# Attention logits moved from TensorE head sums to VectorE on quarter-and-head partitions, with the residual placed in PSUM by ScalarE

## The chip, the cores and the metric

The kernel runs on one core of one Trainium2 chip. The metric is the device time of one execution in microseconds. All data are fp32. A single core runs here, so there is no second die to compare with; "state" says only whether a run was within 1.5% of the fastest of its kernel.

## The reference, cut to what matters

Two bottleneck blocks run one after the other over a batch of 16 images of 1024 channels and 32x32 pixels. The first contains local attention over 3x3 neighbours (8 channels per head, 32 heads), the second a 3x3 convolution.

```python
# block 1
h = relu(bn1(conv1x1(x, w_conv1)))               # 1024 -> 256
q = relu(bnq(conv1x1(h, wq))); k = relu(bnk(conv1x1(h, wk))); v = bnv(conv1x1(h, wv))
kp   = (unfold3x3(k) + pos_h + pos_w).reshape(b, HEADS, d, 9, h, w)
attn = softmax(einsum('bgdhw,bgdkhw->bgkhw', qh, kp), axis=taps)
out  = relu(bnatt(einsum('bgdkhw,bgkhw->bgdhw', unfold3x3(v), attn)))
x1   = relu(bn3(conv1x1(out, w_conv3)) + x)      # 256 -> 1024, residual
# block 2
t = relu(bn(conv1x1(x1, w1))); t = relu(bn(conv3x3(t, w2)))
y = relu(bn(conv1x1(t, w3)) + x1)                # 256 -> 1024, residual
```

## The kernel before

Per image TensorE (PE) goes through six stages: *last_conv* (256 to 1024, ends block 1), *reduce_one*, the first convolution of a later image, a *Winograd* 3x3 convolution, the q/k/v *projection* of the image two ahead, and *expand_last* (256 to 1024, ends block 2). Attention runs beside all this on VectorE (DVE) and ScalarE (ACT). The order of each engine's instructions is settled when the program is built: code yields in the source say how the two strands are traced, and the builder may reorder within the data dependencies.

The logits of a pair of taps: DVE multiplies on channel partitions, PE sums the 8 channels of a head, ACT moves the sums out of PSUM (an *eviction*).

```python
def sums(k0, nk, prods):
    pl = psl.tile([P, 2, JPIX], F32, tag="pl")
    for n in range(NW):
        for j in range(NJ):
            nc.tensor.matmul(pl[j*NH:(j+1)*NH, :nk, :], heads[:, n, :],
                             prods[n][:, :nk, j*JPIX:(j+1)*JPIX], start=(n == 0), stop=(n == NW-1))
    nc.scalar.activation(e[:, k0:k0+nk, :], pl[:, :nk, :], AF.Identity)
...
nc.vector.scalar_tensor_tensor(prod, kp_window, posf[:, n, k], q[:, n], ALU.add, ALU.mult)
...
tree(ALU.max, mx)                                   # over the 9 taps
nc.vector.tensor_tensor(e, e, mx.unsqueeze(1).to_broadcast(...), ALU.subtract)
nc.scalar.activation(e, e, AF.Exp)
```

Both expand stages add the residual on DVE after the matmuls:

```python
def expand_conv(b, wt, src, scale, shift):
    for o in range(NC):                              # 8 tiles of 128 output channels
        xt = xr[b, o]                                # the residual, loaded by DMA
        ps = psum.tile([P, HW], F32, tag="ps")
        ... 4 matmuls into ps, start=(n == 0) ...
        nc.vector.scalar_tensor_tensor(xt, ps, scale(o), xt, ALU.mult, ALU.add)
        nc.scalar.activation(xt, xt, RELU, bias=shift(o), scale=1.0)
        yield o
```

Values go from channel partitions to "quarter of the image, head" partitions by eight DMAs (`vc<-vh`) after the projection. In *expand_last* each tile's output store is followed by the load of a residual of the next image. All these DMAs are issued by one queue, SP's.

Of the kernel before, what the change touches and what calls it, by code (L numbers as in the profile page):

```python
# [12 lines left out]
P = 128  # L13
# [11 lines left out]
XSTREAM = 5  # L25
# [4 lines left out]
HALO = (JROWS + 2) * PW  # L30
G = P // HEAD_DIM
# [28 lines left out]
def sa_bottleneck_kernel(ctx: ExitStack, tc: tile.TileContext, x, w1t, wqkvt, w3t, u1t, u2t, u3t, params, out):  # L60
# [6 lines left out]
    hpool = ctx.enter_context(tc.tile_pool(name="hpool", bufs=4))  # L67
# [3 lines left out]
    psum = ctx.enter_context(tc.tile_pool(name="psum", bufs=3, space=bass.MemoryType.PSUM))  # L71
    psl = ctx.enter_context(tc.tile_pool(name="psl", bufs=2, space=bass.MemoryType.PSUM))
# [23 lines left out]
    uw = dram.tile([NU, P, NW, NU, WID], F32, tag="uw", name="uw")  # L96
    queue, ready = [], []

    def fetch(name, b):

        t = wpool.tile([P, 2048], F32, tag="w", name=f"{name}_{b}")
        if name[0] == "U":
            i = int(name[1])
            nc.sync.dma_start(t, uw[i].rearrange("p m j o -> p (m j o)"))
            ready.append((name, b, t.rearrange("p (m j o) -> p m j o", m=NW, j=NU)))
            return
        src, n = {
            "w1": (w1t, WID), "wqkv": (wqkvt, 3 * WID), "w3": (w3t, C), "u1": (u1t, WID), "u3": (u3t, C)
        }[name]
        chunks = src.shape[0] // P  # L110
        view = t[:, : chunks * n].rearrange("p (c n) -> p c n", n=n)
        nc.sync.dma_start(view, src.rearrange("(c p) n -> p c n", p=P))
        ready.append((name, b, view))
# [35 lines left out]
    pos = const.tile([P, NW, 3, 3], F32, tag="pos", name="pos")  # L149
    for n in range(NW):  # L150
        ph = col("L0_conv_pos_h", 3 * n, 3)
        pw = col("L0_conv_pos_w", 3 * n, 3)
        nc.vector.tensor_tensor(
            pos[:, n],
            ph.unsqueeze(2).to_broadcast([P, 3, 3]),
            pw.unsqueeze(1).to_broadcast([P, 3, 3]),
            ALU.add,
        )
    posf = pos.rearrange("p n i j -> p n (i j)")
# [3 lines left out]
    heads = const.tile([P, NW, NH], F32, tag="heads", name="heads")  # L163
    nc.gpsimd.memset(heads, 0.0)
    for n in range(NW):
        block = heads[:, n, n * G : (n + 1) * G]
        nc.gpsimd.memset(block, 1.0)
        for base, sign in ((0, 1), (HEAD_DIM - 1, -1)):
            nc.gpsimd.affine_select(
                out=block,  # L170
                in_=block,
                compare_op=ALU.is_ge,
                fill=0.0,
                base=base,
                pattern=[[-sign * HEAD_DIM, G]],
                channel_multiplier=sign,
            )

# [67 lines left out]
    def expand_conv(b, wt, src, scale, shift):  # L246

        for o in range(NC):
            xt = xr[b, o]
            ps = psum.tile([P, HW], F32, tag="ps", name="ps")  # L250
            for half in range(2):
                for n in range(NW):
                    nc.tensor.matmul(  # L253
                        ps[:, halves(half)],
                        wt[:, n, o * P : (o + 1) * P],
                        src[:, n, halves(half)],
                        start=(n == 0),
                        stop=(n == NW - 1),
                    )
            nc.vector.scalar_tensor_tensor(xt, ps, scale(o), xt, ALU.mult, ALU.add)  # L260
            nc.scalar.activation(xt, xt, RELU, bias=shift(o), scale=1.0)  # L261
            yield o
# [22 lines left out]
    hidden, queries, values, attended = {}, {}, {}, {}  # L285

    def project(b):

        wqkv = take("wqkv", b)
        h = hidden.pop(b)  # L290
        q = hpool.tile([P, NW, HW], F32, tag="h", name=f"q_{b}")
        for which, name, func in ((0, "bnq", RELU), (1, "bnk", RELU), (2, "bnv", AF.Identity)):
            for n in range(NW):
                ps = psum.tile([P, HW], F32, tag="ps", name="ps")
                at = which * WID + n * P
                for half in range(2):
                    for m in range(NW):
                        nc.tensor.matmul(  # L298
                            ps[:, halves(half)],
                            wqkv[:, m, at : at + P],  # L300
                            h[:, m, halves(half)],
                            start=(m == 0),
                            stop=(m == NW - 1),
                        )
                if which == 0:
                    dst, src = q[:, n, :], ps
                else:
                    dst, src = inside((kp, vh)[which - 1], n), rows(ps)
                nc.scalar.activation(  # L309
                    dst, src, func,  # L310
                    bias=col(f"L0_conv_{name}_b", n), scale=col(f"L0_conv_{name}_s", n),
                )
                yield
        more_weights()
        queries[b] = q

    def relay_values(b):


        vc = apool.tile([P, HEAD_DIM, HALO], F32, tag="vc", name=f"vc_{b}")  # L320
        for n in range(NW):
            flat = vh[:, n].rearrange("p r w -> p (r w)")
            for j in range(NJ):
                at = j * NH + n * G
                nc.sync.dma_start(
                    vc[at : at + G],
                    flat[:, j * JROWS * PW : j * JROWS * PW + HALO],
                )
        values[b] = vc

    def logits(b):

        q = queries.pop(b)
        e = apool.tile([P, KK, JPIX], F32, tag="e", name=f"e_{b}")

        def sums(k0, nk, prods):
            pl = psl.tile([P, 2, JPIX], F32, tag="pl", name="pl")
            for n in range(NW):
                for j in range(NJ):
                    nc.tensor.matmul(  # L340
                        pl[j * NH : (j + 1) * NH, :nk, :],
                        heads[:, n, :],
                        prods[n][:, :nk, j * JPIX : (j + 1) * JPIX],
                        start=(n == 0),
                        stop=(n == NW - 1),
                    )
            nc.scalar.activation(e[:, k0 : k0 + nk, :], pl[:, :nk, :], AF.Identity)

        before = None
        for k0 in range(0, KK, 2):  # L350
            nk = min(2, KK - k0)
            prods = []
            for n in range(NW):
                prod = ppool.tile([P, 2, HW], F32, tag="t", name="prod")
                for k in range(nk):
                    i, j = divmod(k0 + k, 3)
                    nc.vector.scalar_tensor_tensor(  # L357
                        rows(prod[:, k, :]),
                        kp[:, n, i : i + H, j : j + W],
                        posf[:, n, k0 + k : k0 + k + 1],  # L360
                        rows(q[:, n, :]),
                        ALU.add,
                        ALU.mult,
                    )
                prods.append(prod)
                yield 1.28 * nk
            sums(k0, nk, prods)
# [23 lines left out]
    def weighted(b):  # L391

        e, se = weights_of.pop(b)
        vc = values.pop(b).rearrange("p d (r w) -> p d r w", w=PW)
        acc = ppool.tile([P, HEAD_DIM, JPIX], F32, tag="t", name="acc")

        def by_row(t):
            return t.rearrange("p d (r w) -> p d r w", w=W)
# [19 lines left out]
        for n in range(NW):  # L418
            for j in range(NJ):
                at = j * NH + n * G  # L420
                nc.sync.dma_start(a[:, n, j * JPIX : (j + 1) * JPIX], acc[at : at + G])  # L421
# [5 lines left out]
        yield 2.3  # L427
# [5 lines left out]
    ATTEND = 2 * KK * 1.28 + 2.7 + 4.7 + 3.9 + 2.3 + (KK - 1) * 4.6 + 2.3  # L433

    def last_conv(b):
# [3 lines left out]
            lambda o: col("L0_conv_bn3_s", o), lambda o: col("L0_conv_bn3_b", o),  # L439
# [33 lines left out]
    def winograd_conv(b, forms, early):  # L473
# [7 lines left out]
        def products(u, v, js):  # L481
            ps = psum.tile([P, 2, NW * TILES], F32, tag="ps", name="ps")
            for at, j in enumerate(js):
                for n in range(NW):
                    for m in range(NW):
# [4 lines left out]
                            start=(m == 0),  # L490
                            stop=(m == NW - 1),
                        )
            return ps

        def by_row(ap):
# [3 lines left out]
        for i in range(NU):  # L499
# [14 lines left out]
            z = (even, odd)[i] if i < 2 else zpool.tile([P, NW * NT, W], F32, tag="z", name="z")  # L514
            for parity, op in enumerate((ALU.add, ALU.subtract)):
                nc.vector.tensor_tensor(
                    z[:, :, parity::2], by_row(both[parity]), by_row(outer[:, parity]), op
# [15 lines left out]
    def expand_last(b):  # L533

        behind = 2
        for o in expand_conv(
            b, take("u3", b), hidden_one.pop(b),
            lambda o: bn_inv[:, 2 * NW + o : 2 * NW + o + 1],
# [41 lines left out]
    def cycle(b):  # L580
        along(last_conv(b), 2.1)
# [11 lines left out]
        if b + 2 < B:  # L593
            along(project(b + 2), 3.0)
        side.finish()
        if b + 2 < B:
            relay_values(b + 2)
            side.start(attend(b + 2))
        along(expand_last(b), 2.1)
# [20 lines left out]
    relay_values(0)  # L620
    for _ in winograd_weights():
        pass
    for c in range(NC):
# [3 lines left out]
    along(first_conv(2), 3.4)  # L627
    along(project(1), 3.4)
    side.finish()
    relay_values(1)  # L630
# [43 lines left out]
```

## Time and profile before

| | before |
|---|---|
| median of the first comparison | 2785.47 us (2782.49 to 2790.90, 4 runs) |
| profiled span, granted PE clock | 2782.0 us, 0.991 |
| PE busy / idle | 2704.2 / 77.8 us |
| a steady batch | 169.58 us |
| first last_conv starts at | 161.74 us |
| idle PE inside steady batches | 13 starts of the Winograd stage, 1.8 us each |

The prediction below shows the lines. In a line of a timeline the columns are start, time to the end of the last of the group, engine, source line, operation, output and inputs, shape, count, and in brackets the idle time before the group and what ended it. PE is the bound: what does not shorten PE's list or close one of its gaps does nothing.

### The profile page before, as it was taken

How to read it: one execution, taken by the hardware profiler on the slowest of the kernel's cores; microseconds unless marked ns; L12 is line 12 of the kernel's file. 1: busy time of each engine (PE TensorE's matmuls, PEld its weight loads, DVE VectorE, ACT ScalarE, POOL GpSimd, SP SyncE). 2: the span in 40 equal slices, each digit the busy share in tenths (PEclk: the TensorE clock that was granted, in tenths of full speed). 3: DMA queues.
4: the chain of work that ended last, by engine and by line, in shares of the span. 5: the costliest groups of instructions: out<-in, count | busy, mean ns of one | idle time of the engine just before them, and what ended most of it. 6: DMA issues, size and time to landing. Idle time of an engine off the chain costs nothing.

```text
span 2782.0 us, 20993 instructions
## 1 busy us (share of the span) xinstructions
PE 2704.2 (97%) x8192; PEld 1347.8 (48%) x8192; DVE 1944.0 (70%) x1683; ACT 672.0 (24%) x659; POOL 5.0 (0%) x13
## 2 busy tenths in 40 slices
PE   7989999999999999999999999999999999999898
PEld 3435345454544646445464454645546454454545
DVE  3769885867759587595866858677685775958725
ACT  2122312223122221313223122231322313122222
POOL 0000000000000000000000000000000000000000
PEclk9999999999999999999999999999999999999998
DMA  8632645346462554625356353464524546144342
GB/s 313 180 66 72 186 133 157 105 135 184 132 181 82 142 161 147 186 78 151 136 163 171 111 154 115 147 173 135 169 97 139 172 133 196 58 121 152 116 141 91
DMA packets 149970, 395.18 MB, mean 142 GB/s; under 512 B 12912, under 2 KB 78448, under 8 KB 141680
## 3 DMA queue, kind: packets, MB, share of 16 engines
q1 hardware_dynamic: 147712, 387.24, 46.3%
q10 hardware_dynamic: 2160, 6.60, 0.6%
q8 instruction: 65, 1.06, 0.2%
q14 instruction: 33, 0.27, 0.0%
HBM read 283.43 MB, written 71.30 MB: 128 GB/s over the span
## 4 chain that ended last, share of the span: by engine, by line
PE 78%; DVE 13%; DMA 3%; SPq 3%; ACT 2%; issue 1%; ACTq 0%; DVEq 0%
PE ps L253 32%; PE ps L234 16%; PE ps L486 14%; PE ps L298 11%; PE pl L340 5%; DVE term L402 3%; DVE acc L414 3%; SPq L421 3%; DVE v L465 3%; DMA a<-acc 2%; DVE tv L460 1%; DVE acc L416 1%; ACT a L422 1%; DMA g<-in_u2t_dram 1%; ACT vh L447 1%
## 5 line engine op out<-in xcount | busy, mean ns | idle before, releaser
L486 PE MATMUL ps<-v,U 128*128 128x256 f32 x2048 | 454.0, 383 | 36.3 <-ACT h L270 23.8
L357 DVE SCALAR_TENSOR_TENSOR prod<-kp,pos,q 128x1024 f32<-128x1024 f32 x288 | 351.5, 1279 | 167.0 <-ACT kp L309 156.1
L253 PE MATMUL ps<-h,u 128*128 128x512 f32 x1024 | 455.1, 601 | 11.2 <-ACT h L525 11.2
L234 PE MATMUL ps<-x,w 128*128 128x512 f32 x1024 | 445.5, 595 | 11.1 <-DMA w<-in_w1t_dram 11.1
L253 PE MATMUL ps<-a,w 128*128 128x512 f32 x1024 | 453.1, 598 | 2.3 <-DVE r L260 2.3
L234 PE MATMUL ps<-r,u 128*128 128x512 f32 x1024 | 442.4, 592 | 0.0
L486 PEld LDWEIGHTS ps<-v,U 128*128 128x128 f32 x2048 | 391.7, 192 | 103.2 <-ACT h L270 29.0
L298 PE MATMUL ps<-h,wqkv 128*128 128x512 f32 x768 | 337.0, 599 | 10.6 <-ACT kp L309 7.2
L253 PEld LDWEIGHTS ps<-h,u 128*128 128x128 f32 x1024 | 193.8, 192 | 269.6 <-issue 234.4
L234 PEld LDWEIGHTS ps<-x,w 128*128 128x128 f32 x1024 | 195.2, 191 | 257.8 <-issue 256.8
L253 PEld LDWEIGHTS ps<-a,w 128*128 128x128 f32 x1024 | 191.6, 190 | 258.0 <-issue 238.3
L234 PEld LDWEIGHTS ps<-r,u 128*128 128x128 f32 x1024 | 194.4, 190 | 245.2 <-issue 240.8
L260 DVE SCALAR_TENSOR_TENSOR r<-ps,bn_inv,r 128x1024 f32<-128x1024 f32 x128 | 164.2, 1283 | 194.0 <-PE ps L253 194.0
L414 DVE TENSOR_TENSOR acc<-acc,term 128x2048 f32<-128x2048 f32 x128 | 292.4, 2284 | 0.5
L402 DVE TENSOR_TENSOR term<-e,vc 128x2048 f32<-128x2048 f32 x128 | 289.9, 2283 | 0.0
L298 PEld LDWEIGHTS ps<-h,wqkv 128*128 128x128 f32 x768 | 147.5, 192 | 191.7 <-issue 178.7
L261 ACT ACTIVATE r<-r,bn_sh 128x1024 f32<-128x1024 f32 x128 | 146.7, 1148 | 346.8 <-DVE r L260 346.7
L465 DVE TENSOR_TENSOR v<-tv 128x512 f32<-128x512 f32 x256 | 160.4, 686 | 76.1 <-DMA a<-acc 74.8
L260 DVE SCALAR_TENSOR_TENSOR r<-ps,par,r 128x1024 f32<-128x1024 f32 x128 | 161.3, 1269 | 49.5 <-PE ps L253 25.2
L261 ACT ACTIVATE r<-r,par 128x1024 f32<-128x1024 f32 x128 | 145.3, 1144 | 182.2 <-DVE r L260 182.1
L340 PE MATMUL pl<-prod,heads 128*32 128x512 f32 (+1 forms) x1280 | 139.8, 555 | 0.0
L507 DVE TENSOR_TENSOR m<-m,ps 128x512 f32<-128x512 f32 x128 | 82.2, 683 | 81.6 <-ACT m L503 81.6
(61 smaller groups left out, 926.9 us busy)
## 6 DMA issues: line engine op xcount, KB each, us to landing
x<-in_x_dram SPq DMA_DIRECT2D x128, 512.0 KB, 3.3
r<-in_x_dram SPq DMA_DIRECT2D x128, 512.0 KB, 5.4
U<-uw SPq DMA_DIRECT2D x64, 1024.0 KB, 5.1
out_dram<-r SPq DMA_DIRECT2D x128, 512.0 KB, 5.9
vc<-vh SPq DMA_DIRECT2D x128, 170.0 KB, 10.7
w<-in_w1t_dram SPq DMA_DIRECT2D x16, 1024.0 KB, 7.8
w<-in_w3t_dram SPq DMA_DIRECT2D x16, 1024.0 KB, 4.9
u<-in_u1t_dram SPq DMA_DIRECT2D x16, 1024.0 KB, 7.5
```

The costliest lines, as they stand in the source:

```text
L234: nc.tensor.matmul(ps[n][:, halves(half)], wt[:, c, n * P : (n + 1) * P], src[:, halves(half)], start=(c == 0), stop=(c == NC - 1),)
L253: nc.tensor.matmul(ps[:, halves(half)], wt[:, n, o * P : (o + 1) * P], src[:, n, halves(half)], start=(n == 0), stop=(n == NW - 1),)
L260: nc.vector.scalar_tensor_tensor(xt, ps, scale(o), xt, ALU.mult, ALU.add)
L261: nc.scalar.activation(xt, xt, RELU, bias=shift(o), scale=1.0)
L298: nc.tensor.matmul(ps[:, halves(half)], wqkv[:, m, at : at + P], h[:, m, halves(half)], start=(m == 0), stop=(m == NW - 1),)
L340: nc.tensor.matmul(pl[j * NH : (j + 1) * NH, :nk, :], heads[:, n, :], prods[n][:, :nk, j * JPIX : (j + 1) * JPIX], start=(n == 0), stop=(n ...
L357: nc.vector.scalar_tensor_tensor(rows(prod[:, k, :]), kp[:, n, i : i + H, j : j + W], posf[:, n, k0 + k : k0 + k + 1], rows(q[:, n, :]), A ...
L402: nc.vector.tensor_tensor(by_row(dst), rows(e[:, k, :]).unsqueeze(1).to_broadcast([P, HEAD_DIM, JROWS, W]), vc[:, :, i : i + JROWS, j : j ...
L414: nc.vector.tensor_add(acc, acc, t)
L421: nc.sync.dma_start(a[:, n, j * JPIX : (j + 1) * JPIX], acc[at : at + G])
L465: nc.vector.tensor_tensor(v[:, j].rearrange("p n (r w) -> p n r w", w=NT), t[:, :, :, j0 : j0 + 2 * NT - 1 : 2], t[:, :, :, j1 : j1 + 2 * ...
L486: nc.tensor.matmul(ps[:, at, n * TILES : (n + 1) * TILES], u[:, m, j, n * P : (n + 1) * P], v[:, j, m, :], start=(m == 0), stop=(m == NW - 1),
```

## The change

The intent: take the head sums off PE. Query and key are moved to quarter-and-head partitions as the values were, so that a head's 8 channels lie along the free axis and DVE can multiply and add them itself. The position term becomes four differences per head (two rows and two columns relative to the last), computed by four matmuls on PE per image and added on DVE. The residual is put in PSUM by ScalarE ahead of the matmuls (a *seed*), and the scales are multiplied into the weights once, at the start. PSUM goes from 3+2 to 4 buffers. Smaller changes come along: 4 instead of 5 buffers for the input, 3 instead of 4 for `h`, and the attention of one image is finished before the projection of a later one begins. The core of the diff, cut:

```diff
-    psum = ... bufs=3 ...; psl = ... bufs=2 ...
+    psum = ... bufs=4 ...
-    def expand_conv(b, wt, src, scale, shift):
+    def expand_conv(b, wt, src, shift):
+        ahead = []
+        def seed(o):
+            if o < NC:
+                ps = psum.tile([P, HW], F32, tag="ps", name="ps")
+                nc.scalar.activation(ps, xr[b, o], AF.Identity)
+                ahead.append(ps)
+        seed(0)
+        seed(1)
         for o in range(NC):
-            ps = psum.tile(...)
+            ps = ahead.pop(0)
             ... matmuls ...
-                        start=(n == 0),
+                        start=False, skip_group_check=True,
-            nc.vector.scalar_tensor_tensor(xt, ps, scale(o), xt, ALU.mult, ALU.add)
-            nc.scalar.activation(xt, xt, RELU, bias=shift(o), scale=1.0)
+            nc.scalar.activation(xr[b, o], ps, RELU, bias=shift(o), scale=1.0)
+            seed(o + 2)
...
     def project(b):
+        # q, k and v to quarter-and-head partitions, each as soon as it is evicted: 8 DMAs each
+                for j in range(NJ):
+                    nc.sync.dma_start(by_head(halo, n, j), flat[:, ...])
+        # 4 position matmuls (64 columns each), evicted by ScalarE and moved by 4 DMAs
...
     def logits(b):
-        ... products on channel partitions, head sums on PE, eviction on ScalarE ...
+        for k in range(KK):
+            nc.vector.tensor_tensor(by_row(t), by_row(qc), kc[:, :, i:i+JROWS, j:j+W], ALU.mult)
+            nc.vector.tensor_add(t[:, 0:4], t[:, 0:4], t[:, 4:8])
+            nc.vector.tensor_add(t[:, 0:2], t[:, 0:2], t[:, 2:4])
+            nc.vector.tensor_add(e[:, k, :], t[:, 0], t[:, 1])
+            yield 4.6
+        ... two adds of the position terms, broadcast over rows and columns of taps ...
```

## The prediction

> **What bounds the kernel now.** I read the page first, then the timeline of one batch on each engine, then busy time by stage, then the waits.
>
> ```profile
> span 2782.0 us, 20993 instructions
> PE 2704.2 (97%) x8192; PEld 1347.8 (48%) x8192; DVE 1944.0 (70%) x1683; ACT 672.0 (24%) x659; POOL 5.0 (0%) x13
> ...
> PE 78%; DVE 13%; DMA 3%; SPq 3%; ACT 2%; issue 1%; ACTq 0%; DVEq 0%
> ...
> L486 PE MATMUL ps<-v,U 128*128 128x256 f32 x2048 | 454.0, 383 | 36.3 <-ACT h L270 23.8
> L357 DVE SCALAR_TENSOR_TENSOR prod<-kp,pos,q 128x1024 f32<-128x1024 f32 x288 | 351.5, 1279 | 167.0 <-ACT kp L309 156.1
> ...
> L340 PE MATMUL pl<-prod,heads 128*32 128x512 f32 (+1 forms) x1280 | 139.8, 555 | 0.0
> ```
>
> PE's busy time is 97% of the span: its idle time is at most 78 us, 60 by my count of gaps. So a saving is either PE work or one of those gaps; DVE (70%) and ACT (24%) matter only where PE waits for them. The granted clock is 0.991.
>
> A steady batch takes 169.58 us (projection starts at 1112.88 and 1282.46), and thirteen of the sixteen batches are such. PE's timeline of one:
>
> ```profile
> 1112.88 20.76 PE L298 MATMUL ps<-h,wqkv 128*128 128x512 f32 x48
> 1133.48 10.46 PE L253 MATMUL ps<-h,u 128*128 128x512 f32 x24
> 1143.87 1.92 PE L340 MATMUL pl<-prod,heads 128*32 128x512 f32 x16
> 1145.73 7.13 PE L253 MATMUL ps<-h,u 128*128 128x512 f32 x16
> ...
> 1258.18 24.44 PE L486 MATMUL ps<-v,U 128*128 128x256 f32 x112 [1.82 <-ACT h L270]
> ```
>
> Starts differ by 20.60 us for 48 projection matmuls: 429 ns each is the true pitch (the "mean 600 ns" overlaps). The head sums stand in PE's stream; 16 take 1.86 us. The one idle gap is 1.82 us at the start of the Winograd stage. On ACT, 25.40 us of waiting for the a<-acc transfers and then two a-activations (1252.09 to 1257) stand ahead of the evictions of h that PE wants.
>
> The queue and DMA decide one step below:
>
> ```profile
> 1134.09 5.15 SPq L325 DMA_DIRECT2D vc<-vh  x7
> 1141.25 5.55 SPq L541 DMA_DIRECT2D out_dram<-r  x3
> 1153.89 0.34 SPq L88 DMA_DIRECT2D r<-in_x_dram  x1
> ...
> 1133.48:1163.40 29.92, 29.92 (x94) 12.14 (x93) 20.21 (x17) 9.33 (x10) 0.00 (x0) 1.00 0.94 229
> ```
>
> The first residual of the next batch is issued 12.6 us after the first output store, because the store must land first; in that stage the DMA share is 0.94.
>
> [...] 16 instructions in 1.86 us, 116 ns each, against 429. [...] At N = 2048 [...] the trace has 2284. [...] the rows with pointers have 1148 (from SBUF) and 1195 to 1209 (from PSUM), so I take 1.15 us. [...]
>
> **The change part by part.**
>
> *Head sums leave PE.* 80 instructions per batch, 8.77 us of PE by stage sums, 16 batches: -140 us.
>
> *Position products join it.* Per batch 4 fp32 matmuls, each two instructions as everywhere in this trace: 8 x 429 ns / 2 side by side = 1.7 us, plus about 0.3 for switching: 2.0 x 16 = +32 us. The weight scaling at the start adds 32 instructions of 128 columns, a quarter of 429 each: +4.
>
> *DVE's work is exchanged, not cut.* Out: 351.5 us of prod and 164.2 + 161.3 = 325.5 us of the residual adds, together 677, or 42.3 per batch. In, per tap: 2.28 (2048 wide) + 1.22 + 0.69 + 0.42 = 4.6 us, nine times 41.4, plus two position adds of 1.76: 44.9. DVE goes from 120.35 to about 123 us per batch. But attention can no longer begin at 11.5 us into the projection: it must wait for q and k to be moved to the new partitions. The k transfers are like the vc ones (170 KB, 10.7 us to landing), the last issued about 18 us in: start at about 27. DVE then has some 135 us for 123: it fits, with attention ending near the end of the next first conv, as now (a<-acc issued at 1245.20, first conv ends at 1252.75).
>
> *ACT.* Seeds 16 x 1.15 = 18.4, less head-sum evictions (43.5/16 = 2.7), plus 1.2 for positions: 41.4 becomes 59 us per batch. In an expand stage it is relu 1.2 + seed 1.15 = 2.35 us per 3.43 us tile. It fits. Every tile is seeded two ahead with four PSUM buffers, so I expect no wait inside a stage.
>
> *Waits removed.* The a-activations are placed 15 us later and there is a fourth PSUM buffer: the 1.8 us gap goes, 13 x 1.8 = 24 us. The 7.24 us wait of the second projection for kp goes too. -31 us.
>
> *Waits gained, start.* Attention of batch 0 begins 74 us in rather than 59.6 and takes 41.4 + 3.5 + 2.9 + 2.5 + 3.5 (exp, table) + 4.5 + 37.7 + 2.2, about 98 us: 172. The transfers and activations of a add 11: the first last_conv starts at 183 instead of 161.7. +22 us.
>
> *Waits gained, each batch.* DMA work in and after the projection rises: 1024 packets of 1 KB for q (6.7 us of all 16 engines, as a<-acc takes), 1024 of 1360 bytes for k (11.5, as vc), 512 for positions (3.3). It begins at 5 us, where DMA is idle now (share 0.19 in the projection), but with vc and a weight load the backlog lasts to about 46 us instead of 38. So the first store lands at about 49 us instead of 41 and residual 0 at about 53. Now the residual is wanted after a tile's matmuls, afterwards before them: seed 0 of the next last_conv is wanted at 50 and done at 54. I choose 4 us for 13 batches: +52.
>
> *Sum.* 2782 - 140 + 36 - 31 + 22 + 52 - 1 (the last tile loses its DVE step) = 2720; the unprofiled median is 2.8 us above the profiled span: **2723 us**, 2.2% less.
>
> **The rivals.**
> (a) *No wait on seeds*: the transfers fit in the idle DMA of the projection. For it: the share of 0.19 there. Against: 0.94 right after. Without the 52 us: about 2670.
> (b) *Seeds and relus collide on ACT*: if the seeds of a stage queue behind the last eviction of the stage before, PE waits 1.2 + 1.15 + about 0.2 us at each of 32 stage starts, +83 us; about 2805 with (c)'s wait, 2755 in its place. Against: ACT is mostly idle, and instruction order here already differs from the source (a first term stands inside the tree of sums), so seeds can be placed early.
> (c) *ACT blocks on exp*: ACT is in order; if exp was placed for an earlier DVE than the real one (k lands late), relus and seeds of last_conv stand behind it. Now exp waits only 2.1 us for DVE. 3 us a batch would be +40 us: 2763.
> (d) *DVE becomes the bound*: 123 of 165 us, idle only while k is moved. If k lands 10 us later than I think, Winograd forms come late and PE waits up to that long: near 2800.
>
> **Range and chances.** With all head-sum savings kept and no new wait in the batches it is 2670; a little less if the start costs less: low 2655. With one more wait of 5 to 6 us a batch it is about 2795. The 2% border, 2729, lies next to my figure; (a) pulls down, (b) to (d) up, and the change looks tuned as a whole (yields, buffers), which favours (a). Faster 0.52, within 2% 0.43, slower 0.05.
>
> **What would show it.** PE busy about 2600 us and no head sums; projection plus positions about 22.5 us; DVE about 123 us a batch with an idle stretch of about 25 us from the Winograd end until k lands; last_conv of a steady batch starting with a wait of about 4 us on a seed that waited for r<-in_x_dram; the first last_conv at about 183 us; no wait on h at the Winograd start; a batch of about 164.5 us instead of 169.6. It is wrong if a batch takes 161 (no seed wait) or above 168 (stage-start or exp waits on ACT), or if the position products run one after another (3.4 us a batch, +24 us).

## The result, and the profile after

The changed kernel took 3200.30 us (3196.59 to 3202.18, 4 runs), against 2785.47 for the kernel before in the same rounds: ratio 1.1485, 95% interval 1.1464 to 1.1506. Ratios in this document are the mean time of one kernel's fast runs over the mean of the other's of the same rounds, so not quite the ratio of the medians quoted. The time is far outside the predicted range.

From the page of the changed kernel (in a group's line: busy time, mean ns of one, then the engine's idle time just before the group and what ended most of it):

```profile
span 3198.2 us, 19613 instructions
...
PE 2632.5 (82%) x7072; PEld 1347.0 (42%) x7072; DVE 1959.8 (61%) x1771; ACT 893.6 (28%) x851; POOL 5.0 (0%) x11
...
L289 PE MATMUL ps<-a,w 128*128 128x512 f32 x1024 | 476.3, 628 | 442.5 <-ACT ps L280 442.5
L407 DVE TENSOR_TENSOR prod<-qc,bnk 128x2048 f32<-128x2048 f32 x144 | 323.9, 2287 | 423.4 <-DMA bnk<-kp 252.7
...
L435 ACT ACTIVATE e<-e 128x2304 f32<-128x2304 f32 x16 | 34.0, 2122 | 432.8 <-DVE e L434 432.8
```

PE's busy time fell by 71.7 us, and still the span rose by 416.2, so PE's idle time rose by 487.9. Of that, 442.5 us stand in one row: *last_conv*'s matmuls waiting for ScalarE's seeds. And ScalarE waited almost the same total, 432.8 us, for DVE ahead of exp. The timeline of one batch shows how the two belong together. First PE:

```profile
1326.62 1.94 PE L379 MATMUL ps<-q,pos 128*64 128x512 f32 x8
...
1335.46 27.63 PE L289 MATMUL ps<-h,u 128*128 128x512 f32 x64
1394.04 29.13 PE L289 MATMUL ps<-a,w 128*128 128x512 f32 x64 [30.95 <-ACT ps L280]
```

*expand_last* ends at 1363.1, and *last_conv* begins 30.95 us later. ScalarE in that stretch:

```profile
1363.18 1.11 ACT L297 ACTIVATE r<-ps,bn_sh 128x1024 f32<-128x1024 f32 x1 [2.38 <-PE ps L289]
1390.95 2.12 ACT L435 ACTIVATE e<-e 128x2304 f32<-128x2304 f32 x1 [26.65 <-DVE e L434]
1392.98 2.90 ACT L280 ACTIVATE ps<-r 128x1024 f32<-128x1024 f32 x3
```

After the last ReLU of *expand_last* ScalarE's next instruction is exp; it stands there for 26.65 us until DVE has finished the logits, and only then do three seeds run, at once. DVE, meanwhile, started its logits late and then never paused:

```profile
1343.77 4.50 DVE L407 TENSOR_TENSOR prod<-qc,bnk 128x2048 f32<-128x2048 f32 x2 [28.23 <-DMA bnk<-kp]
...
1388.36 2.56 DVE L434 TENSOR_TENSOR e<-e,mx 128x2304 f32<-128x2304 f32 x1
```

It waited 28.23 us for the keys, and the subtraction that exp needs ended at 1390.9. The residuals were not the cause: in SP's list the first of them is issued at 1363.44, behind the eight values and three output stores,

```profile
1338.87 8.84 SPq L369 DMA_DIRECT2D bnv<-vh  x8
...
1350.29 3.42 SPq L595 DMA_DIRECT2D out_dram<-r  x3
1363.44 0.34 SPq L88 DMA_DIRECT2D r<-in_x_dram  x1
```

and the trace has it landed at 1367.74, some 25 us before the first seed ran.

The built order of ScalarE's instructions agrees (not a profile; a piece of the list of ACT instructions in the program built from the changed kernel):

```
L297 Activation r_6_2396<-ps,bn_sh 128x1024
L297 Activation r_7_2398<-ps,bn_sh 128x1024
L435 Activation e_2862<-e_2862 128x2304
L280 Activation ps<-r_0_2889 128x1024
L280 Activation ps<-r_1_2904 128x1024
```

Exp is ahead of every seed of the next *last_conv*, and ScalarE keeps to its list: in those 26.65 us it ran none of the seeds, although the residual of the first was there from 1367.74.

**The bill.** PE idle: +442.5 at *last_conv* (one wait of 39.1, thirteen of 30.6 to 32.0), +71.5 in the start (88.8 us of waits against 17.3), -23.7 for the thirteen Winograd waits, which are gone. (The first wait for weights, 11 to 12 us in both, is left out of the start.) Together +490, against +487.9 measured from busy times. PE busy: -71.7. A steady batch takes 194.0 us.

There is a smaller cost inside PE's busy time. Here are the wait, the *last_conv* after it and the next stage (columns: stretch, its length, busy PE, PEld, DVE, ACT and POOL, each with its count, then the granted clock, the DMA share and GB/s):

```profile
1362.00:1394.00 32.00, 1.08 (x3) 0.19 (x1) 29.71 (x28) 4.17 (x4) 0.00 (x0) 0.57 0.75 288
1394.00:1423.00 29.00, 28.96 (x64) 12.84 (x65) 29.00 (x17) 14.41 (x14) 0.00 (x0) 0.95 0.00 1
1423.00:1450.50 27.50, 27.50 (x66) 12.18 (x65) 2.92 (x2) 2.32 (x2) 0.00 (x0) 1.00 0.11 38
```

64 matmuls of one shape take 29.0 us after the wait and 27.5 one stage on, and the clock is 0.95 against 1.00. The trace's clock record stands at half from 1366.17, 3.1 us after the last matmul, to 1396.89, 2.9 us after the first one. In that slow beginning matmuls start 854 ns apart, afterwards 429. The ends of matmuls are modelled, so this is a reading of starts.

### The profile page after: what moved, and what is told of

The parts are those of the page before. It is cut to its first block, busy times and chain, and to the rows that moved or that the text cites. A ratio compares the mean times of both kernels' runs of the same rounds, so it can differ in the third digit from the quotient of the medians.

```text
span 3198.2 us, 19613 instructions
## 1 busy us (share of the span) xinstructions
PE 2632.5 (82%) x7072; PEld 1347.0 (42%) x7072; DVE 1959.8 (61%) x1771; ACT 893.6 (28%) x851; POOL 5.0 (0%) x11
## 5 line engine op out<-in xcount | busy, mean ns | idle before, releaser
L289 PE MATMUL ps<-a,w 128*128 128x512 f32 x1024 | 476.3, 628 | 442.5 <-ACT ps L280 442.5
L407 DVE TENSOR_TENSOR prod<-qc,bnk 128x2048 f32<-128x2048 f32 x144 | 323.9, 2287 | 423.4 <-DMA bnk<-kp 252.7
L289 PEld LDWEIGHTS ps<-a,w 128*128 128x128 f32 x1024 | 206.0, 203 | 712.6 <-ACT ps L280 454.7
L260 PE MATMUL ps<-x,w 128*128 128x512 f32 x1024 | 448.7, 598 | 38.2 <-DMA x<-in_x_dram 26.7
L510 DVE TENSOR_TENSOR tv<-vh 128x1088 f32<-128x1088 f32 x64 | 82.4, 1287 | 460.1 <-ACT vh L497 459.5
L453 DVE TENSOR_TENSOR term<-e,bnv 128x2048 f32<-128x2048 f32 x128 | 289.9, 2284 | 0.0
L280 ACT ACTIVATE ps<-r 128x1024 f32<-128x1024 f32 x256 | 257.5, 1021 | 13.8 <-DVE m L558 3.8
L297 ACT ACTIVATE r<-ps,par 128x1024 f32<-128x1024 f32 x128 | 142.6, 1114 | 244.9 <-PE ps L289 184.8
L297 ACT ACTIVATE r<-ps,bn_sh 128x1024 f32<-128x1024 f32 x128 | 142.5, 1113 | 203.4 <-PE ps L289 203.4
L410 DVE TENSOR_TENSOR prod<-prod 128x1024 f32<-128x1024 f32 x144 | 170.3, 1220 | 0.0
L435 ACT ACTIVATE e<-e 128x2304 f32<-128x2304 f32 x16 | 34.0, 2122 | 432.8 <-DVE e L434 432.8
```

The lines of the kernel that those rows point to most:

```text
L260: nc.tensor.matmul(ps[n][:, halves(half)], wt[:, c, n * P : (n + 1) * P], src[:, halves(half)], start=(c == 0), stop=(c == NC - 1),)
L280: nc.scalar.activation(ps, xr[b, o], AF.Identity)
L289: nc.tensor.matmul(ps[:, halves(half)], wt[:, n, o * P : (o + 1) * P], src[:, n, halves(half)], start=False, stop=(n == NW - 1), skip_grou ...
L297: nc.scalar.activation(xr[b, o], ps, RELU, bias=shift(o), scale=1.0)
L407: nc.vector.tensor_tensor(by_row(t), by_row(qc), kc[:, :, i : i + JROWS, j : j + W], ALU.mult)
L410: nc.vector.tensor_add(t[:, 0:4], t[:, 0:4], t[:, 4:8])
```

## The experiments

All give correct results but for one that is meant not to (said there). Each was run beside the kernel before on the same chip.

### 1. Exp queued behind the seeds

Theory A: exp's place in ScalarE's list makes the wait. Rival B: the seeds wait for something of their own (residuals, PSUM buffers), and exp only hides it. Edit: exp is made to stand behind the newest seed that has been traced.

```diff
+                newest[0] = nc.scalar.activation(ps, xr[b, o], AF.Identity)   # in seed()
...
-        nc.scalar.activation(e, e, AF.Exp)
+            with tc.issue_after(newest[0].ins):
+                nc.scalar.activation(e, e, AF.Exp)
```

> Edit: exp is queued on ACT behind the newest seed that was traced before it; nothing else. Theory (order): the 31 us wait of each last_conv is ACT standing at exp, in front of the seeds, until DVE has finished the logits. Then the wait falls to what the residual transfers leave, about 5 to 7 us (residual 0 lands 55 us after the projection's start, the stage could start at 50, plus a seed of 1.0); a batch takes 166 to 169 us instead of 194 and the kernel about 3200 - 14 x 26 = 2835 us (2800 to 2870). Rival (transfers): the seeds themselves come late because of the added relays; then the wait stays over 20 us and the kernel over 3080. Rival (late attention): the wait moves to the next point that needs attention; a batch stays over 185.

Measured: 2848.02 us, ratio 1.0238 (1.0213 to 1.0264): 352 us of the 415 between the medians came back with this one edit, as the theory expected. The waits at *last_conv* fell from 442.5 to 95.8 us in all. ScalarE at such a start:

```profile
1400.74 1.11 ACT L299 ACTIVATE r<-ps,bn_sh 128x1024 f32<-128x1024 f32 x1 [2.38 <-PE ps L291]
1405.74 1.03 ACT L282 ACTIVATE ps<-r 128x1024 f32<-128x1024 f32 x1 [3.88 <-DMA r<-in_x_dram]
...
1428.36 2.12 ACT L441 ACTIVATE e<-e 128x2304 f32<-128x2304 f32 x1 [3.54 <-DVE e L436]
```

Exp still comes when DVE is ready, but nothing that PE wants is behind it. What remains, 5.7 to 7.4 us a batch, is B: the seed waits 3.88 us for its residual. That is the wait that I had predicted, and it was hidden below the greater one.

### 2. No seeds at all

The residual is added by DVE in both stages, as before the change, but the rest of the change stays. If seeds are the fault, this should give the gain without the wait.

```diff
-        seed(0); seed(1)
-            ps = ahead.pop(0)            ... start=False
-            nc.scalar.activation(xr[b, o], ps, RELU, ...); seed(o + 2)
+            ps = psum.tile(...)          ... start=(n == 0)
+            nc.vector.tensor_tensor(xt, ps, xt, ALU.add)
+            nc.scalar.activation(xt, xt, RELU, bias=shift(o), scale=1.0)
```

> Edit: residual added by VectorE after the matmuls in both expand stages, as before the change (scales stay folded into the weights, all else of the change stays). ACT still has exp ahead of the relus of last_conv. Theory (order): PE no longer waits for ACT at last_conv, so that wait goes to 0; the relus stand behind exp, so a wait comes at reduce_one, which reads them: exp is ready about 78 + 10 us (eight adds ahead of it on DVE) after the projection's start and reduce_one could start at 77.5, so 10 to 16 us. A batch 171 to 179, kernel 2890 to 3000. Rival (relays and late attention are the cost, seeds are innocent): a batch stays at 185 to 194, kernel over 3080.

Measured: 3316.07 us, ratio 1.1912 (1.1894 to 1.1930), slower than the change itself: a clear miss. A batch takes 201.3 us. By its number the rival's forecast (over 3080 us) came true; the lines show what the wait is. PE in one batch:

```profile
1608.32 13.90 PE L280 MATMUL ps<-a,w 128*128 128x512 f32 x32
1661.40 15.78 PE L280 MATMUL ps<-a,w 128*128 128x512 f32 x32 [39.19 <-DVE r L287]
```

DVE's timeline there:

```profile
1654.24 2.56 DVE L424 TENSOR_TENSOR e<-e,mx 128x2304 f32<-128x2304 f32 x1
1658.99 1.23 DVE L416 TENSOR_TENSOR tree<-e 128x1024 f32<-128x1024 f32 x1 [2.19 <-ACT e L425]
1660.13 1.22 DVE L287 TENSOR_TENSOR r<-ps,r 128x1024 f32<-128x1024 f32 x1
```

PE fills the four PSUM buffers (32 of its 64 matmuls) and stops for 39.19 us, because the residual adds now stand in DVE's list behind the whole logits. It is the same fault on another engine: a short instruction that PE wants, behind a long chain that began late. Taking the seeds away does not take away the late start of the logits.

### 3. Seeds in expand_last only

*last_conv* adds on DVE, *expand_last* keeps its seeds, and exp is tied behind the newest ReLU. Edit: `seeded` is passed to the two stages as False and True, with the add of experiment 2 where it is False.

> Edit: seeds stay in the last expand stage; last_conv adds its residual on VectorE; exp is queued behind the newest relu traced before it. Theory (order plus late residuals): both parts of the wait go, the exp in front of the seeds and the residual that is wanted a tile earlier; a batch takes 161 to 164 us, kernel 2745 to 2800, level with the kernel before, because the start still loses about 75 us more than before. Rival (DVE becomes the bound with 133 us a batch and a late start): batch over 168 with waits at the Winograd stage for forms, kernel over 2840.

Measured: 2993.59 us, ratio 1.0753 (1.0737 to 1.0769). A miss again, with half the wait. PE's timeline in one batch:

```profile
1325.11 15.48 PE L292 MATMUL ps<-a,w 128*128 128x512 f32 x32 [16.09 <-DVE r L301]
```

DVE's timeline there:

```profile
1321.36 2.56 DVE L440 TENSOR_TENSOR e<-e,mx 128x2304 f32<-128x2304 f32 x1
1323.84 4.61 DVE L301 TENSOR_TENSOR r<-ps,r 128x1024 f32<-128x1024 f32 x4
```

Four adds stand behind the subtraction, which ends the logits. I had not asked, before either run, where the adds would stand in DVE's list; the bracket answers it. With seeds, only exp has to be moved out of the way; with adds, the logits themselves.

### 4. The start reworked

On top of experiment 3: the weight scaling takes residual buffers instead of those of the products, the first projection is traced after the preparation of the Winograd weights, and the residuals of batch 0 are loaded after the second image's first convolution.

```diff
+        diag = rpool.tile([P, NC, P], F32, tag="r", name="diag")      # one buffer for all 8 diagonals
...
-    along(project(0), 0.0)          # ahead of the Winograd weights
+    along(project(0), 0.0)          # behind them
-    for c in range(NC): load_residual(0, c)
     side.start(attend(0)); along(first_conv(1), 3.4)
+    for c in range(NC): load_residual(0, c)
```

> Edit: e3, and at the start the Winograd weights are traced before the first projection, the scaled weights use the residual buffers instead of the product buffers, and the first residuals are loaded after the second first_conv. Theory: the start loses 15 us to scaled weights that wait for a buffer, 27 us to input loads behind residual loads in the queue, and attention 0 starts 22 us late; the first last_conv begins near 185 us instead of 216, and the kernel is 25 to 45 us faster than e3: 2700 to 2770. Rival (the start is bound by attention 0 alone): under 10 us gained.

Measured: 2973.92 us, ratio 1.0684 (1.0666 to 1.0702): 20 us less than experiment 3 by the medians, a little under the 25 to 45 that were expected. (The times named there built on experiment 3's expectation, which had failed.) The first *last_conv* began at 191.7 us instead of 215.8. The wait for scaled weights (15 us) is gone, that for the second image's input fell from 27 to 16.

### 5. Only the order of the values' transfers

Values are wanted last in attention, yet their eight transfers stand ahead of the stores and residuals in SP's queue. Edit: from the third image on they are queued behind the last residual load. Exp is left alone: nothing in the code of the attention, the seeds or the ReLUs is changed.

```diff
-                        nc.sync.dma_start(dst, src)                 # v: at once
+                    later.extend(relays)                             # v, b > 1
...
+            with tc.issue_after(last_residual_load):
+                for dst, src in later: nc.sync.dma_start(dst, src)
```

> Edit: the changed kernel, only that the eight transfers that relay v (1.36 MB a batch, from batch 2 on) are queued behind the residual loads of the next batch; exp is not tied. In the built program exp then stands behind seven of the eight relus of last_conv by itself: with the v relays ahead of the stores and residuals, the builder's order had taken the residuals to come after exp. Theory (order plus DMA backlog): the residual lands about 11 us earlier (some 44 us after the projection's start, wanted at 50), so the wait at last_conv falls from 31 us (6 us in e1) to under 1.5; v arrives at about 72 to 75 us, before its first use at about 80. A batch 161 to 163 us, kernel 2740 to 2780. Rival (v now arrives too late and DVE ends later): waits at the Winograd stage of over 3 us, batch over 166, kernel over 2820.

Measured: 2803.11 us, ratio 1.0070 (1.0055 to 1.0085); 397 us of the 415 are gone, though the time is above what was expected: a batch takes 165.7 us, not 161 to 163, and the wait at *last_conv* is 2.18 us, not under 1.5. Two things happened. The residual was issued at 41.88 us into the projection and landed at 46.25, instead of 50.65 and 54.95. And the builder, given this other order, by itself put exp behind ReLU 6 of *last_conv*, 15 instructions later than in the changed kernel. So where exp stands is no part of the source; it came out of the order of transfers. Why the builder chose as it did, no trace shows.

What is left of waits per batch, on PE's timeline:

```profile
1322.78 7.14 PE L542 MATMUL ps<-v,U 128*128 128x256 f32 x32 [2.22 <-ACT m L560]
...
1382.24 7.97 PE L290 MATMUL ps<-a,w 128*128 128x512 f32 x14 [2.18 <-ACT ps L281]
```

ScalarE's timeline ahead of the second of them:

```profile
1380.15 1.11 ACT L298 ACTIVATE r<-ps,bn_sh 128x1024 f32<-128x1024 f32 x1 [2.38 <-PE ps L290]
1381.16 2.91 ACT L281 ACTIVATE ps<-r 128x1024 f32<-128x1024 f32 x3
```

The seed follows the last ReLU of the stage before: 1.11 and 1.03 us in a row after the last matmul, the collision of the prediction's rival (b). The 2.22 us are a Winograd eviction behind an a-activation (one of the attention's two normalising activations) that waits for its transfer.

### 6 and 7. The start again, and another queue

Experiment 5 plus the start of experiment 4:

> Edit: e5 plus the start of e4 (weights traced earlier, scaled weights in residual buffers, first residuals after the second first_conv). e4 gained 20 us over e3; the same here: 2715 to 2760, and 15 to 30 us under e5.

Measured: 2782.08 us, ratio 1.0001 (0.9981 to 1.0021), 21 us less than experiment 5 by the medians, as in experiment 4, but above the 2715 to 2760 that were expected, because experiment 5 was. The second image's later input loads were issued from GpSimd's queue in addition:

```diff
-            nc.sync.dma_start(t, x[b, c*P:(c+1)*P, :])
+            queue_of = nc.gpsimd if b == 1 and c >= XSTREAM else nc.sync
+            queue_of.dma_start(t, x[b, c*P:(c+1)*P, :])
```

> Edit: e6 plus the last four input loads of batch 1 issued by GpSimd, so that they don't stand behind the 28 relays in the SP queue. The 16 us wait of PE for them in e4 goes; since the first last_conv waits for attention 0 anyway (about 190 us), only part of it comes out: 0 to 15 us under e6, 2705 to 2755.

Measured: 2785.88 us, ratio 1.0008 (0.9992 to 1.0025): no gain. The wait for those inputs fell from 20.7 to 1.2 us, and other waits of the start took its place: PE waits 12.8 us for a product of VectorE that it did not wait for before, and 38.1 us for evictions of queries instead of 28.3.

### 8. Half the multiplications, on purpose wrong

If exp's readiness sets the wait in the changed kernel, shorter logits must shorten it by as much, with every order and every transfer as it was. Edit: for 8 of the 9 taps only 4 of the 8 channels are multiplied and the first tree step is left out. The result is wrong (relative error 0.041).

> Wrong result on purpose: the changed kernel with eight of the nine taps of the logits over half of each head (1024 instead of 2048 wide, first fold left out), about 2.2 us of VectorE less for each, 17.6 a batch, all ahead of exp. ACT's order in the steady batches is the same as in the changed kernel. Theory (exp stands ahead of the seeds, and waits for DVE): the wait at last_conv falls by just that, from 31 to 13 to 14 us; kernel about 2930 to 2960. Rival (the seeds wait for transfers, or PE for something else): the wait stays over 25 us, kernel over 3100.

Measured: 2931.38 us in its only run (its state is therefore unknown). PE's timeline in one batch:

```profile
1265.89 30.27 PE L289 MATMUL ps<-a,w 128*128 128x512 f32 x64 [13.47 <-ACT ps L280]
```

ScalarE's timeline just before it:

```profile
1262.80 2.12 ACT L437 ACTIVATE e<-e 128x2304 f32<-128x2304 f32 x1 [9.17 <-DVE e L436]
```

PE's wait fell from about 31 to 13.1 to 13.9 us, as expected. With the order the same, it follows DVE's time.

### 9. The seeds of last_conv ahead of the last two ReLUs

On experiment 6: in the last two tiles of *expand_last* the seed of the next *last_conv* runs before the tile's ReLU. Four PSUM buffers allow that.

```diff
+            if o >= NC - 2 and following is not None:
+                early = seed(o + 2)                  # first two tiles of the next last_conv
+                with tc.issue_after(early.ins):
+                    nc.scalar.activation(xr[b, o], ps, RELU, bias=shift(o), scale=1.0)
```

> The level version (v's relays late, start reworked) with one edit: while expand_last works on its last two tiles, ScalarE first seeds the next last_conv's first two PSUM tiles and only then does the ReLUs of tiles 6 and 7. In the level version 13 last_conv starts wait 2.18 us each for a seed that stands behind the last ReLU (1.11 + 1.03 us, my rival b). Theory (only the order of the last ReLU and the seed makes that wait): it goes, 13 x 2.2 = 28 us, 2782 to about 2754 us. Rival (the residual is what is late: it lands 46.3 us after the projection start, ReLU 6 runs at about 47): the wait stays at 1 to 2 us, now with a DMA behind the seed, and the time stays above 2770 us. The Winograd starts still wait 1.4 to 2.3 us.

Measured: 2743.54 us, ratio 0.9852 (0.9837 to 0.9867). Experiment 6 had fourteen waits of 2.18 us at *last_conv*; the first is left (2.23 us), the thirteen others are gone, so the residual was there in time. The gain is 39 us by the medians, more than the 28 of these waits. In the profiled runs, of which experiment 6's was its slowest, the span fell by 49.3 us: PE's idle time by 30.0 us and its busy time by 19.3, at a granted clock of 0.980 instead of 0.973. The same matmuls ran a little faster, 16.7 us of it in *last_conv*'s row (460.5 against 443.8 us on the two pages). The traces show why: in experiment 6 the clock record stands at half for 3.41 us just after nine of the fourteen waits of 2.18 us, and those nine stages take 29.43 us, the other five 27.73. (Experiment 5's timeline has such a pair too: after waits of 2.18 us the stage at 1217.17 took 27.73 us, that at 1382.24 took 29.43.) So each of the nine waits in experiment 6 cost 1.70 us beyond their own length.

### 10. The attention's normalising activations behind the Winograd evictions

On experiment 9: the two a-activations, which wait for transfers, are made to stand behind the four evictions that PE wants.

```diff
-        yield 15.0
-        for n in range(NW): nc.scalar.activation(a[:, n, :], a[:, n, :], RELU, ...)
+        yield 1000.0                                  # left to the end of the Winograd stage
+        with tc.issue_after(newest[0].ins):           # the newest Winograd eviction
+            for n in range(NW): nc.scalar.activation(a[:, n, :], a[:, n, :], RELU, ...)
```

> The same, and the attention's two normalising activations queued on ScalarE behind the four evictions of the Winograd convolution instead of ahead of three of them. In the level version 13 Winograd convolutions stop 1.4 to 2.3 us (mean 1.9) for such an eviction, which stands behind an activation that waits for the last DMA of the accumulators. Theory: those 13 x 1.9 = 24 us go too, about 2730 us, 0.98 of the kernel before. Rival: what waits behind the moved activations (the relays of the attention's output, the next query evictions) becomes late, and 5 to 20 us come back as waits at the projection or positions.

Measured: 2708.21 us (2707.03 to 2709.22, 5 runs), ratio 0.9728 (0.9714 to 0.9741). This version beats both kernels. The 35 us under experiment 9, where 24 were expected, are 27.8 of PE's idle time and 6.3 of its busy time in the profiled runs. The engines' busy times on its page:

```profile
PE 2591.8 (96%) x7072; PEld 1332.9 (49%) x7072; DVE 1955.4 (72%) x1771; ACT 890.3 (33%) x851; POOL 5.0 (0%) x11
```

PE's timeline of a batch:

```profile
1247.26 27.79 PE L559 MATMUL ps<-v,U 128*128 128x256 f32 x128
...
1297.56 27.63 PE L294 MATMUL ps<-h,u 128*128 128x512 f32 x64
1325.02 27.63 PE L294 MATMUL ps<-a,w 128*128 128x512 f32 x64
```

ScalarE's timeline at the border of the two expand stages, where the seed (1319.37) now comes before the last two ReLUs, tiles 6 and 7:

```profile
1318.36 1.11 ACT L307 ACTIVATE r<-ps,bn_sh 128x1024 f32<-128x1024 f32 x1 [2.32 <-PE ps L294]
1319.37 1.02 ACT L283 ACTIVATE ps<-r 128x1024 f32<-128x1024 f32 x1
1321.79 1.11 ACT L305 ACTIVATE r<-ps,bn_sh 128x1024 f32<-128x1024 f32 x1 [1.40 <-PE ps L294]
```

No PE row has a bracket: a steady batch has no wait. It takes 160.16 us (one *last_conv* starts at 1325.02, the one before at 1164.86), where the prediction gave 161 for "no seed wait". PE is busy for 2591.8 us, 40.7 less than in the changed kernel for the same 7072 matmuls: that is my estimate of what the slow clock after the waits cost there. 32.4 us of it are in *last_conv*'s row (476.3 against 443.9 us on the two pages).

### 11. A control: the same repair in the kernel before

How much of 0.973 is the change, and how much a repair that the old kernel could have had? The edit of experiment 10 is put in the kernel before. With it `side.finish()` moves up, so that the attention is finished ahead of the next projection, as in the changed kernel; so the control does not change ScalarE's order alone.

> A control: the kernel BEFORE with only the last repair of the best version, its two normalising activations queued on ScalarE behind the four evictions of the Winograd convolution. In the kernel before, 13 Winograd convolutions start 1.8 us late because evictions stand behind these activations. Theory (the waits hang on ScalarE's order alone, with the old logits as with the new): those 13 waits go, 13 x 1.8 = 24 us, about 2760 us, ratio 0.992; the rest of the best version's gain (0.973) is then the change's own. Rival (the old kernel needs the activations early, for last_conv of the next batch but one): the waits come back elsewhere and the ratio is 0.998 to 1.002.

Measured: 2757.85 us, ratio 0.9903 (0.9887 to 0.9920). All thirteen Winograd waits are gone. The engines' busy times on its page:

```profile
PE 2700.2 (98%) x8192; PEld 1348.9 (49%) x8192; DVE 1943.1 (70%) x1683; ACT 673.3 (24%) x659; POOL 5.0 (0%) x13
```

Against this fairer rival the best version gains 49.6 us by the medians, 1.8%; the two were not run in one call. Their profiled spans differ by 51.6 us: PE's busy time is 108.4 us less, and its idle time 56.8 us more (113.5 against 56.7), some 52 of it in the start, by the waits listed in the two traces. How much of that part could still be removed stays open. A likely reason, not tested, is that the new logits need keys and queries moved before anything can begin, and that the first attention has little to hide behind.

## Why the prediction was wrong

**Right, by the traces.** Projection with positions took 22.67 us (predicted 22.5), the position products 1.94 us (2.0): they do run two side by side, in pairs that start 6 to 7 ns apart. DVE is busy 1959.8 / 16 = 122.5 us a batch (123). It waits 28.2 us for the keys (25) and starts the logits 31.0 us into the projection (27). The first residual landed at 54.95 us into the projection (53). The Winograd waits went, as said. A seed takes 1.03 us and a ReLU 1.11 (1.15 and 1.2). A batch without waits takes 160.16 us (161).

**The step that failed** is "Waits gained, each batch". I put 4 us there, for a seed that waits for its residual. That wait exists, as experiment 1 shows (5.7 to 7.4 us on PE, so a little under-sized). But in the changed kernel ScalarE's list has exp ahead of all seeds of *last_conv*, and the wait is 31 us. Thirteen times 31 us plus a first of 39 make the 442.5; the clock cost about 41 more (the estimate from the 2632.5 and 2591.8 us of experiment 10); the sum had 52. The rest of the 477 us between prediction and measurement is nearly all in the start, where PE's waits grew by 71.5 us and the sum had 22. (A slip besides: the prediction's own terms give a batch of 165.0 us, not 164.5.)

**Rival (c) named this mechanism and sized it ten times too small.** It said that ScalarE is in order and that exp, "placed for an earlier DVE", would hold up relus and seeds of *last_conv*, for 3 us a batch. I had the numbers for a better size in the prediction itself: logits start 27 us after the projection begins and DVE then works for about 45 + 3 + 3 us, so exp is ready at some 77 us; *last_conv* wants its seed at 50. If exp stands ahead of that seed, the wait is 27 us plus exp and a seed, 30. Instead I took the 2.1 us that exp waits in the kernel before and added a little. Experiments 1, 5 and 8 show the mechanism from three sides: moving exp, moving only transfers so that exp moves (and the residual comes earlier), and moving only exp's readiness.

**"Instruction order already differs from the source, so seeds can be placed early"** was my argument against rival (b), and it was taken the wrong way: reordering placed exp early, not the seeds. Rival (b) is real too, 2.18 us per *last_conv* in experiment 5, and it took an explicit tie to remove (experiment 9). Rival (a), no seed waits, is what experiment 10 had to be made into; rival (d), DVE as the bound, did not come: DVE is idle where it waits for keys and PE has no gap in a steady batch of experiment 10.

**The start was under-sized.** I gave it +22 us; the first *last_conv* began at 216.5 us instead of the predicted 183. I had left out the weight scaling's wait for buffers (15.3 us), the inputs of the second image behind 28 transfers and 8 residual loads in one queue (26.7), an eviction of queries and one of keys behind a-activations (12.6 and 3.3 us), and, after that *last_conv*, an eviction of queries that waits for VectorE's accumulation (18.6; queries and `acc` share a pool of four buffers). Experiments 4 and 6 each took back some 20.

**The range.** It treated each rival as a few us a batch. When a rival says that an in-order engine stops for another, its size is the difference of the two engines' times at that point, and it can be the length of a stage.

## What to carry to other kernels

When a change makes one chain start later, list every instruction that stands behind that chain's consumer in an in-order engine's list, and size the wait from the clock times of both, not from the wait that is there now. Read the built order before believing the source order, and tie the few instructions that the bound engine wants (seeds, evictions) ahead of those that wait for a long chain; here three such edits (the values' transfers later, the seeds earlier, the normalisation later) and a reworked start turned 1.149 into 0.973 with the arithmetic unchanged. And give the old kernel the same repair before crediting the change: a third of the gain was the repair.

## What the traces show of issue, clock and seeds

- How far ahead one queue can issue these runs do not show: the limit that they show is the program's own. In the changed kernel the transfers issued at 1350.29, 1351.84 and 1353.38 began within 0.1 us of the landings at 1350.23, 1351.78 and 1353.30 of the eighth before each. The trace has the reason: SP's transfers use eight semaphores in turn, and each issue first waits for the one that the eighth before it raises on landing. So at most eight of the 28 small transfers are under way at once (eight is also the most of all 1104 in the trace), and everything behind them in the queue is late, which is why their order moved the residual by 8.7 us (experiment 5).
- In experiment 6 the clock went to half after nine of the fourteen waits of 2.18 us, 0.3 to 1.4 us after the matmuls had begun again, for 3.41 us. In the kernel before it did so after none of the thirteen waits of 1.6 to 2.1 us. With a gap of 30.6 us or more in each of 14 batches PE's busy time for the same matmuls was 40.7 us longer than without gaps (2632.5 against 2591.8), 1.3% of the span.
- 256 seeds per execution were written by ScalarE in the changed kernel and in experiments 1, 5 to 7, 9 and 10, and every result was correct. That shows that it worked in this program, not that it is safe elsewhere.
